# A four-layer block kernel: GpSimd's list in the scan taken in program order, decays moved to the end of a slot, softplus in other buffers, a residual moved; in the latent attention, roots on ScalarE and key masks on GpSimd

## The chip, the cores and the metric

The kernel runs on one core of a Trainium2 chip. A core has TensorE (PE, matrix products and transposes, with separate weight loads PEld), VectorE (DVE), ScalarE (ACT), GpSimd (POOL), SyncE (SP, which here only issues transfers) and 16 DMA engines. Each engine works through its own list of instructions in order and waits at semaphores for the others. The metric is device time in microseconds (us); lower is better.

## The reference, cut to what matters

The input is 32 sequences of 256 tokens with 128 features. Four layers follow each other, each with two halves; every half normalizes, scales and shifts with values drawn from a conditioning vector, does its work, and adds the gated result to `x`. The change touches the first half of layer 0 (a selective scan), the first half of layer 3 (attention whose keys and values come from a narrow latent), and the normalization that opens the second half of layer 3.

```python
h = _layernorm(x, axis=-1) * (1 + ca) + sa
x = x + ga * _L0_attn_ref(h, ...)              # in here:
    xn = (x - mu) * rsqrt(var + EPS) * ln_w + ln_b
    xp = xn @ proj_W.T + proj_b
    def branch(W, b):
        u = softplus(xp @ W.T + b)
        dbc = u @ deltaBC_W.T                  # delta (64), B (16), C (16)
        delta = softplus(delta @ dt_W.T + dt_b)
        h[t] = exp(delta * A) * h[t-1] + (delta * u) * B   # 16 states a feature
        return sum over states of h[t] * C + u * D
    z = xp * sigmoid(xp)
    return branch(fconv) * z + branch(bconv) * z + skip
...
x = x + ga * _L3_attn_ref(h, ...)              # in here:
    q = x @ Wq + bq;  latent = x @ Wl + bl     # latent: 32 features
    k = latent @ Wk + bk;  v = latent @ Wv + bv
    out = softmax(q k^T * SCALE) v;  return out @ Wo + bo
x = x + gb * _L3_ffn_ref(h, ...)               # gated products with blockwise FP4 rounding
```

## The kernel before

The tokens lie in 16 tiles `b` of 512. A stage runs after another; within one, a Python agenda says what is recorded in which slot, and slots are then recorded in order. How that becomes each engine's list differs by engine. Matrix products and transposes (`mm`, `tr`) are kept in program order. In the scan ScalarE's activations are too (`strict_act`); VectorE's and GpSimd's lists there are ordered by a scheduler, by what it takes to be ready first. In the latent attention VectorE is kept in program order (`nc.vector.on`, all shown at line 304), and ScalarE's and GpSimd's lists are the scheduler's.

**The scan** (`scan_layer`). A tile takes 16 slots, and eight groups `p` of two slots: four groups for each of the two branches, four states a group. In slot 2p (`scan_even`) TensorE spreads the inputs into PSUM (`dB`, one buffer of it), and VectorE runs four `tensor_tensor_scan` of 512 (line 875) with the four `decay` tiles. The states then go back through TensorE transposes (`hT`, one PSUM buffer), a ScalarE copy (`hsT`) and products with the spread C (`y<-hsT,Cd`, `scan_weigh`) into one PSUM tile, which ScalarE copies to `yT` after the last group. The decays are exponentials on ScalarE, two a slot (`scan_decay`, ten tiles). A `hT` half of group p is recorded in slot 2p+2 or 2p+3, the decays and the weighing directly behind it, ahead of everything else of the slot.

Everything else prepares later tiles: two normalizations (`norm_rows`, `scan_roots` with the root as Ln and Exp on ScalarE and a Newton step on GpSimd, `norm_scale`), the projections, softplus in two halves (`soft_start` on VectorE, tiles `sp_r` and `sp_m` with one buffer each; `soft_end` on ScalarE and GpSimd), the rows of B and C with a turn through DRAM (`scan_rows`, `far`, `Xc`, and the GpSimd copy `Xr`), their spread forms `Bd` and `Cd` (four GpSimd products each), and after a tile its end: `scan_end` (VectorE `y`, GpSimd `y*z` and `y+h`) and `residual` (VectorE, two instructions into `x`). All side products share one PSUM buffer, `tp`.

**The latent attention** (`latent_attention` in `attention`). A tile takes 16 slots. In each slot TensorE forms one block of scores for the row maximum (`S<-kx,q`, reduced by VectorE into `mt`) and one block for the exponential (`S<-qa,kx`, read by ScalarE into `E`), and the products with the values (`po`). `S` has three PSUM buffers, taken in turn. Ahead of a tile, in slots -14 to -2, come its normalization (`norm_rows`, then `norm_place` with the root by integer start and four Newton steps on VectorE), the latent, the queries, the keys (`keys`: a product of 32 rows with the key weights into a buffer of `S`, then four ScalarE activations that add the bias and mask alternate heads into `kx`) and the values. Behind it come the residual and the same normalization for the next half (`mlp_norm`, tile `fx`) with FP4 rounding on VectorE. The last tile's second normalization is done in the stage after, `fp4_mlp`, where ScalarE is in program order.

Of the kernel before, what the change touches and what calls it, by code (L numbers as in the profile page):

```python
# [30 lines left out]
P = 128  # L31
NSEQ, SEQ = 32, 256
NB = 16
# [107 lines left out]


def rows(v):

    v = np.asarray(v, np.float32).reshape(1, -1)
    return np.broadcast_to(v, (P, v.shape[1]))
# [29 lines left out]
def packs(d):  # L176
# [91 lines left out]
    k.add("Wl", g["Wl"])  # L268
    k.add("Wk", spread(g["Wk"]))
    k.add("Wo", gathered(g["Wo"]))  # L270
    k.add("Wv", np.concatenate([g["Wv"], g["bv"][None]], 0))
    k.add("bq", spread(g["bq"][None])[0].T)
    k.add("kb", key_bias(g["bk"]))
    k.add("bo", col(g["bo"]))
# [32 lines left out]
class Engines:  # L307
    def __init__(self, tc):
        self.nc = tc.nc
        self.vector = InOrder(tc, tc.nc.vector)  # L310

    def __getattr__(self, name):
# [3 lines left out]
class Program:  # L316
# [161 lines left out]

    def norm_newton(self, mv, v, r):


        pool = self.nc.gpsimd
        t = self.wk("ln_t", (P, 4))
        pool.tensor_tensor(t, r, r, ALU.mult)
        pool.tensor_tensor(t, t, v, ALU.mult)
        pool.tensor_scalar(t, t, -0.5, 1.5, ALU.mult, ALU.add)
        pool.tensor_tensor(r, r, t, ALU.mult)
        shift = self.wk("ln_m", (P, 4))
        pool.tensor_tensor(shift, mv[:, :, 0], r, ALU.mult)
        pool.tensor_scalar(shift, shift, -1.0, None, ALU.mult)  # L490
        return r, shift

    def norm_scale(self, xn, r, shift):
# [162 lines left out]
    def scan_layer(self, w):  # L656
# [7 lines left out]
        with ExitStack() as ctx:  # L664
            self.pools(
                ctx, {"dB": 1, "hT": 1, "y": 1, "tp": 1},
                h=4, z=3, dl=3, duT=3, bc=3, xn=1, ln_xn=1, xp=1, y=1, yT=1, rows=1, Xc=1, du=1, sg=1, hsT0=1, hsT1=1, sp_m=1, sp_r=1, Xr=1, mw=1,
            )
            self.strict = self.strict_act = True
            wk = self.wk  # L670
# [16 lines left out]
            def put(t, f, *args):  # L687
                agenda.setdefault(t, []).append((f, args))
# [5 lines left out]
            for n in (1, 2, 3):  # L694
                put(8 * n - 52, lambda n=n: s.update({("mw", n): self.mod_load(n)}))
                put(8 * n - 46, lambda n=n: self.mod_layer(n, s["mw", n], self.ps("y", (P, 6, NSEQ))))
            for p in range(-1, 8 * NB + 3):
                put(2 * p, self.scan_even, s, p)
                put(2 * p + 1, self.scan_odd, s, p)
            for b in range(NB):  # L700
                a = s[b] = {"b": b}
                T = 16 * b
                put(T, self.clear_regions)


                for o, n, src in ((T - 44, 1, lambda a: self.x[a["b"]]), (T - 36, 2, lambda a: a["h"])):
                    put(o, lambda a, n=n, src=src: a.update({("st", n): self.norm_rows(src(a), self.nc.gpsimd)}), a)
                    put(o + 1, lambda a, n=n: self.scan_roots(a, n), a)
                    put(o + 3, lambda a, n=n: self.norm_scale(a["st", n][0], *a["r", n]), a)
                put(T - 40, self.scan_norm_out, a)  # L710
                put(T - 32, self.scan_norm_out2, s, a)
                put(T - 21, self.scan_proj, s, a)
                put(T - 20, self.scan_gate, s, a)
                put(T - 19, self.scan_gate2, s, a)
                for br in (0, 1):
                    o = T + 8 * br
                    put(T - 19 + 6 * br, self.scan_u, s, a, br)
# [12 lines left out]
            self.strict = self.strict_act = False  # L730

# [29 lines left out]

    def soft_start(self, src, bias):

        m, r = self.wk("sp_m"), self.wk("sp_r")
        self.nc.vector.tensor_scalar(r, src, bias, 0.0, ALU.add, ALU.max)
        self.nc.vector.scalar_tensor_tensor(m, r, -2.0, src, ALU.mult, ALU.add)
        return m, r, bias

    def soft_end(self, out, m, r, bias):
        self.act(m, m, AF.Exp, bias=bias)  # L770
        self.act(m, m, AF.Ln, bias=1.0)
        self.nc.gpsimd.tensor_tensor(out, m, r, ALU.add)

    def scan_u(self, s, a, br):
        w = s["w"]
        pu = self.ps("tp")
        self.mm(pu, w.conv[:, br, :], a["xp"])
        a["soft"] = self.soft_start(pu, w.vec[:, 3 + br : 4 + br])

    def scan_u2(self, s, a, br):  # L780
        a["u", br] = self.wk("u")
        self.soft_end(a["u", br], *a["soft"])

    def scan_delta(self, s, a, br):
        pt = self.ps("tp")
        self.mm(pt, s["wd"], a["u", br])
        a["soft"] = self.soft_start(pt, s["w"].vec[:, 5:6])

# [4 lines left out]
    def scan_rows(self, s, a, br):  # L793
# [10 lines left out]
        nc.sync.dma_start(Xc, far.rearrange("n k r -> k n r"))  # L804
        a["Xc"] = self.wk("Xr", (16, 4, 32, 4))
        nc.gpsimd.tensor_copy(a["Xc"].rearrange("k g r n -> k g n r"), Xc.rearrange("k (g n) r -> k g n r", g=4))
        dl = a["dl", br] = self.wk("dl")
        self.soft_end(dl, *a["soft"])
        a["du"] = self.wk("du", (P, 4, 4, 32))
        dq, uq = (t.rearrange("p (q i r) -> p q i r", **cut) for t in (dl, u))  # L810
        nc.gpsimd.tensor_tensor(self.by_chunk(a["du"]), dq, uq, ALU.mult)
        if br:
            a["uu"] = self.wk("uu")
            nc.gpsimd.tensor_tensor(a["uu"], a["u", 0], u, ALU.add)
            nc.gpsimd.tensor_scalar(a["uu"], a["uu"], s["w"].vec[:, 6:7], None, ALU.mult)

# [39 lines left out]
    def scan_even(self, s, p):  # L856
# [48 lines left out]
    def scan_weigh(self, s, p, h):  # L905
# [7 lines left out]
        for i in (0, 1):  # L913
            for q in range(4):
# [5 lines left out]
                    stop=p % 8 == 7 and h == 1 and i == 1,  # L920
                )

    def scan_sum(self, s, a):
# [624 lines left out]
    def keys(self, h, w, bias):  # L1548
# [5 lines left out]
        for x in (0, 1):  # L1554
            for j in (0, 1):
# [5 lines left out]
                    scale=self.c.half[:, j : j + 1],  # L1561
                )
        return k4

# [904 lines left out]
    def latent_attention(self, w):  # L2469
        nc, c = self.nc, self.c  # L2470
        self.mlp_start()
        with ExitStack() as ctx:
# [7 lines left out]
            def before(b, tiles):  # L2480
                t = tiles[b] = {"vz": self.vzs[4 * (b % 2) : 4 * (b % 2) + 4]}

                def head():
                    t["st"] = self.norm_rows(self.x[b])
                    t["norm"] = self.norm_place(*t["st"])

# [16 lines left out]
                def k():  # L2503
                    t["k4"] = self.keys(t["lat"][:32, :], w.Wk, w.kb)

# [316 lines left out]
```

## Time and profile before

| what | us |
|---|---|
| ten runs, median | 6576.51 |
| ten runs, lowest to highest | 6569.2 to 6587.16 |
| the profiled execution, its own time | 6578.39 |
| its span, first to last instruction | 6575.4 |
| first group of scans to the last one of layer 0 | 111.1 to 1079.6 |
| a scan tile in the steady part (scans of group 0 to those of the next tile) | 62.4 |
| the latent attention | about 5488 to 6317 |

A profile row names engine, source line, operation, output and inputs, and a count; in brackets stands how long the engine had been idle before and what ended that. Line 392 is any matrix product, 396 any transpose, 399 any activation through the helper `act`, 304 any VectorE instruction kept in program order; so rows are told apart by the tiles. A wait belongs to the engine that waited. An engine's busy share is a mean over eight stages with different limits, so the two touched stages are read on their own.

### The profile page before, as it was taken

What the parts mean: (1) busy time and instruction counts of PE and PEld (TensorE: products, weight loads), DVE (VectorE), ACT (ScalarE), POOL (GpSimd) and SP (SyncE); (2) the same over time, 40 slices, a digit from 0 to 9 for tenths busy, and PEclk for the clock granted to TensorE, in tenths of its full rate; (3) what the DMA queues carried; (4) which work ended last, traced back from release to release, by engine and by line L of the source; (5) the groups of instructions that cost most, each with busy time, mean ns of one, the idle gap of its engine ahead of it and who ended that gap; (6) DMA issues with size and microseconds to landing.
All of it is one profiled execution on the core that took longest, in us unless ns stands there. A gap on an engine that the chain in (4) does not pass through costs nothing. (4 is left out here: it accounts for less than half of the span.)

```text
span 6575.4 us, 132969 instructions
## 1 busy us (share of the span) xinstructions
PE 5813.9 (88%) x54369; PEld 3298.0 (50%) x54369; DVE 4311.9 (66%) x9937; ACT 3490.6 (53%) x5026; POOL 2660.5 (40%) x2882
## 2 busy tenths in 40 slices
PE   6788886999799999999999777999799998999987
PEld 4555555567465565555655434555322223444444
DVE  4777776621566666665665654888677774777779
ACT  5888884333344444444444432444488885554532
POOL 4555553565444444444543453444245452000000
PEclk7999997899899999999999878999899998998998
DMA  1110110144000000000000101111144441000010
GB/s 63 42 42 29 42 42 33 39 124 130 17 5 6 6 6 5 7 6 5 7 2 2 48 14 28 29 30 27 39 95 91 91 92 36 17 18 17 17 34 30
DMA packets 175877, 232.19 MB, mean 35 GB/s; under 512 B 46567, under 2 KB 95967, under 8 KB 175010
## 3 DMA queue, kind: packets, MB, share of 16 engines
q1 hardware_dynamic: 124880, 126.50, 7.5%
q0 software_dynamic: 26992, 56.62, 3.5%
q10 hardware_dynamic: 23394, 40.58, 1.6%
q8 instruction: 426, 6.98, 0.4%
q14 instruction: 185, 1.52, 0.1%
HBM read 88.22 MB, written 74.97 MB: 25 GB/s over the span
## 5 line engine op out<-in xcount | busy, mean ns | idle before, releaser
L304 DVE TENSOR_REDUCE mt<-S 128x4 f32<-128x1024 f32 (+2 forms) x768 | 756.0, 999 | 508.6 <-PE S L392 505.5
L1438 ACT ACTIVATE E<-S 128x1024 f32<-128x1024 f32 x448 | 458.5, 1024 | 545.9 <-PE S L392 511.1
L875 DVE TENSOR_TENSOR_SCAN hs<-decay,dB 128x512 f32<-128x512 f32 x512 | 582.9, 1203 | 91.7 <-PE dB L392 77.1
L399 ACT ACTIVATE hid<-S,bigw 128x1024 f32<-128x1024 f32 x512 | 537.3, 1111 | 125.5 <-PE S L392 125.3
L1912 POOL TENSOR_SCALAR_AFFINE_SELECT E<-E 128x1024 f32<-128x1024 f32 x320 | 348.7, 1092 | 587.8 <-ACT E L1911 587.3
L304 DVE TENSOR_TENSOR E<-S,cst 128x1024 f32<-128x1024 f32 x320 | 391.2, 1223 | 291.6 <-PE S L392 291.1
L392 PE MATMUL S<-qa,kx 32*128 32x256 f32 x4096 | 538.7, 383 | 34.5 <-DVE mt L304 34.0
L392 PE MATMUL S<-kx,q 32*128 32x512 f32 (+1 forms) x2048 | 528.0, 610 | 17.0 <-ACT kx L1556 16.1
L1911 ACT COPY E<-S 128x1024 f32<-128x1024 f32 x320 | 323.5, 1011 | 327.0 <-PE S L392 315.1
L2459 POOL TENSOR_TENSOR acc<-acc,ye 128x512 f32<-128x512 f32 x256 | 344.5, 1346 | 362.4 <-DVE ye L304 319.6
L392 PEld LDWEIGHTS S<-qa,kx 32*128 32x128 f32 x4096 | 341.5, 190 | 140.2 <-DVE mt L304 104.4
L392 PE MATMUL S<-qG,f 32*128 32x512 f32 x2560 | 368.4, 645 | 47.4 <-DVE E L304 47.4
L392 PE MATMUL S<-hm,bigw 32*128 32x512 f32 x2048 | 340.3, 656 | 25.2 <-ACT hid L399 25.2
L399 ACT ACTIVATE hsT<-hT 128x1024 f32<-128x1024 f32 x256 | 260.8, 1019 | 157.1 <-PE hT L396 156.1
L399 ACT ACTIVATE decay<-dl,A 128x510 f32<-128x510 f32 x512 | 339.1, 715 | 0.0
L396 PE MATMUL hT<-cst,hs 128*128 128x128 f32 x2048 | 295.6, 290 | 22.5 <-ACT hsT L399 21.4
L392 PE MATMUL po<-hid,bigw 128*32 128x512 f32 x2048 | 277.3, 614 | 30.2 <-DVE ye L304 30.2
L1787 ACT ACTIVATE E<-S 128x768 f32<-128x768 f32 (+1 forms) x192 | 169.0, 880 | 237.8 <-PE S L392 237.8
L392 PE MATMUL po<-E,vz 128*32 128x256 f32 x4096 | 294.3, 372 | 0.3 <-ACT oc L1458 0.2
L304 DVE TENSOR_TENSOR ye<-po,gb 128x512 f32<-128x512 f32 x256 | 176.0, 688 | 176.7 <-PE po L392 106.2
L392 PE MATMUL po<-E,vzl 128*32 128x128 f32 x8192 | 276.8, 276 | 0.0
L396 PEld LDWEIGHTS hT<-cst,hs 128*128 128x128 f32 x2048 | 235.0, 147 | 82.4 <-ACT hsT L399 65.1
(530 smaller groups left out, 12930.0 us busy)
## 6 DMA issues: line engine op xcount, KB each, us to landing
gb<-gT SPq DMA_DIRECT2D x256, 256.0 KB
regions<-zeros ACTq DMA_DIRECT2D x16, 2048.0 KB
rx<-far SPq DMA_DIRECT2D x64, 256.0 KB
expert_rows<-eo SPq DMA_DIRECT2D x39, 256.0 KB
xin<-in_x SPq DMA_DIRECT2D x16, 256.0 KB
out<-out SPq DMA_DIRECT2D x16, 256.0 KB
xTd<-xT SPq DMA_DIRECT2D x15, 256.0 KB
xT<-xTd SPq DMA_DIRECT2D x15, 256.0 KB
```

The lines of the kernel that those rows point to most:

```text
L304: return lambda *args, **kw: self.tc.keep_in_program_order(op(*args, **kw))
L392: return self.tc.keep_in_program_order(self.nc.tensor.matmul(out, lhsT, rhs, start=start, stop=stop, **kw))
L396: return self.tc.keep_in_program_order(self.nc.tensor.transpose(out, in_, self.c.ident[:k, :k]))
L399: ins = self.nc.scalar.activation(*args, **kw)
L875: nc.vector.tensor_tensor_scan(hs[:, :, n], decay, dB[:, :, n], 0.0, ALU.mult, ALU.add)
L1438: nc.scalar.activation(e, src, AF.Exp, scale=scale)
L1787: nc.scalar.activation(e, src, AF.Exp, scale=1.0 / math.sqrt(8))
L1911: nc.scalar.copy(e, src)
L1912: nc.gpsimd.affine_select(e, e, [[0, 8], [1, P]], ALU.is_ge, 0.0, base=0, channel_multiplier=-1)
L2459: nc.gpsimd.tensor_tensor(a["acc"], a["acc"], ye, ALU.add)
```

## The change

In the scan, GpSimd's instructions are recorded in program order (`nc.gpsimd.on`). In each slot the two decays and the weighing products are recorded last, behind the side work; the decays are then those of half a group later than before. The copy `yT` is recorded directly behind the last weighing. Softplus writes its first half into the tile that takes the result (`u` or `dl`), so `sp_r` is gone, and `sp_m` has two buffers. The copy `Xr` and the scaling of `uu` are recorded one and two slots after their old place. The residual is recorded in slot T + 25 in place of T + 23.

In the latent attention and `mlp_norm`, the normalization takes its root from Ln and Exp on ScalarE, one Newton step on GpSimd, and four GpSimd instructions to apply it. The key weights carry the bias as a 33rd row; ScalarE copies the product once, and two GpSimd products mask it.

```diff
-    k.add("Wk", spread(g["Wk"]))
+    k.add("Wk", np.concatenate([spread(g["Wk"]), key_row(g["bk"])], 0))
-    k.add("kb", key_bias(g["bk"]))
...
+        self.gpsimd = InOrder(tc, tc.nc.gpsimd)
...
-    def norm_newton(self, mv, v, r):
+    def norm_newton(self, mv, v, r, shifted=True):
...
+        if not shifted:
+            return r, None
...
+    def norm_apart(self, xn, mv, v):
+
+        r = self.norm_roots(v)
+        yield
+        r, _ = self.norm_newton(mv, v, r, False)
+        for n in range(4):
+            self.nc.gpsimd.tensor_scalar(
+                xn[:, n, :], xn[:, n, :], mv[:, n, 0:1], r[:, n : n + 1], ALU.subtract, ALU.mult
+            )
+        yield
...
-                h=4, z=3, dl=3, duT=3, bc=3, xn=1, ln_xn=1, xp=1, y=1, yT=1, rows=1, Xc=1, du=1, sg=1, hsT0=1, hsT1=1, sp_m=1, sp_r=1, Xr=1, mw=1,
+                h=4, z=3, dl=3, duT=3, bc=3, xn=1, ln_xn=1, xp=1, y=1, yT=1, rows=1, Xc=1, du=1, sg=1, hsT0=1, hsT1=1, Xr=1, mw=1,
             )
-            self.strict = self.strict_act = True
+            self.strict = self.strict_act = nc.gpsimd.on = True
...
-            for p in range(-1, 8 * NB + 3):
+            behind = {}
+            for p in range(-2, 8 * NB + 3):
                 put(2 * p, self.scan_even, s, p)
                 put(2 * p + 1, self.scan_odd, s, p)
+                behind[2 * p] = (p + 1, 1), (p - 2, 1)
+                behind[2 * p + 1] = (p + 2, 0), (p - 1, 0)
...
+                    put(o - 13, self.scan_chunks, s, a)
...
-                put(T + 18, self.scan_sum, s, a)
+                put(T - 4, lambda a: nc.gpsimd.tensor_scalar(a["uu"], a["uu"], w.vec[:, 6:7], None, ALU.mult), a)
                 put(T + 21, self.scan_end, s, a)
-                put(T + 23, lambda a: self.residual(0, 0, a["b"], a["y"]), a)
+                put(T + 25, lambda a: self.residual(0, 0, a["b"], a["y"]), a)
             for t in sorted(agenda):
                 for f, args in agenda[t]:
                     f(*args)
+                if t in behind:
+                    decay, sums = behind[t]
+                    self.scan_decay(s, *decay)
+                    self.scan_weigh(s, *sums)
...
-    def soft_start(self, src, bias):
-        m, r = self.wk("sp_m"), self.wk("sp_r")
-        self.nc.vector.tensor_scalar(r, src, bias, 0.0, ALU.add, ALU.max)
-        self.nc.vector.scalar_tensor_tensor(m, r, -2.0, src, ALU.mult, ALU.add)
-        return m, r, bias
+    def soft_start(self, out, src, bias):
+        m = self.wk("sp_m")
+        self.nc.vector.tensor_scalar(out, src, bias, 0.0, ALU.add, ALU.max)
+        self.nc.vector.scalar_tensor_tensor(m, out, -2.0, src, ALU.mult, ALU.add)
+        return out, m, bias
...
-        nc.gpsimd.tensor_copy(a["Xc"].rearrange("k g r n -> k g n r"), Xc.rearrange("k (g n) r -> k g n r", g=4))
...
-            nc.gpsimd.tensor_scalar(a["uu"], a["uu"], s["w"].vec[:, 6:7], None, ALU.mult)
+
+    def scan_chunks(self, s, a):
+        Xc, to = a["rows by chunk"], self.wk("Xr", (16, 4, 32, 4))
+        self.nc.gpsimd.tensor_copy(to.rearrange("k g r n -> k g n r"), Xc.rearrange("k (g n) r -> k g n r", g=4))
+        a["Xc"] = to
...
         self.scan_turned(s, p - 1, 0)
-        self.scan_decay(s, p + 1, 0)
-        self.scan_weigh(s, p - 2, 1)
...
         self.scan_turned(s, p - 1, 1)
-        self.scan_weigh(s, p - 1, 0)
-        self.scan_decay(s, p + 1, 1)
...
+        if p % 8 == 7 and h == 1:
+            self.scan_sum(s, a)
...
+    def masked_keys(self, lat, w):
+
+        pk = self.ps("S", (P, 2, TB))
+        for x in (0, 1):
+            self.mm(pk[:, x, :], w[:, x, :], lat)
+        both = self.wk("kk", (P, 2, TB))
+        self.nc.scalar.copy(both, pk)
+        k4 = self.wk("kx", (P, 2, 2, TB))
+        for x in (0, 1):
+            self.nc.gpsimd.tensor_tensor(
+                k4[:, x],
+                both[:, x, :].unsqueeze(1).to_broadcast([P, 2, TB]),
+                self.c.half.unsqueeze(2).to_broadcast([P, 2, TB]),
+                ALU.mult,
+            )
+        return k4
...
-                    t["st"] = self.norm_rows(self.x[b])
-                    t["norm"] = self.norm_place(*t["st"])
+                    t["st"] = self.norm_rows(self.x[b], nc.gpsimd)
+                    t["norm"] = self.norm_apart(*t["st"])
...
-                    t["k4"] = self.keys(t["lat"][:32, :], w.Wk, w.kb)
+                    t["k4"] = self.masked_keys(t["lat"], w.Wk)
...
-        a["st"] = self.norm_rows(self.x[a["b"]], tag="fx")
-        a["norm"] = self.norm_place(*a["st"])
+        a["st"] = self.norm_rows(self.x[a["b"]], self.nc.gpsimd, "fx")
+        a["norm"] = self.norm_apart(*a["st"])
```

More of the change, by code (lines that the diff above doesn't have):

```diff
@@ L140, in key_bias, with key_row @@
     return out.reshape(4, P).T.reshape(P, 2, 2)
+def key_row(b):
+    full = spread(np.asarray(b)[None]).reshape(1, 2, 8, 16)
+    full[:, :, :, 8] = 1.0
+    return full.reshape(1, 2, P)
 def rows(v):
@@ L729, in scan_layer @@
                     f(*args)
-            self.strict = self.strict_act = False
+                if t in behind:
+                    decay, sums = behind[t]
+                    self.scan_decay(s, *decay)
+                    self.scan_weigh(s, *sums)
+            self.strict = self.strict_act = nc.gpsimd.on = False
     def scan_roots(self, a, n):
@@ L760, in scan_gate2, with soft_end @@
         self.nc.gpsimd.tensor_tensor(a["z"], a["z"], a["xp"], ALU.mult)
-    def soft_start(self, src, bias):
-        m, r = self.wk("sp_m"), self.wk("sp_r")
-        self.nc.vector.tensor_scalar(r, src, bias, 0.0, ALU.add, ALU.max)
-        self.nc.vector.scalar_tensor_tensor(m, r, -2.0, src, ALU.mult, ALU.add)
-        return m, r, bias
-    def soft_end(self, out, m, r, bias):
+    def soft_start(self, out, src, bias):
[3 more added lines that the diff above has]
+        return out, m, bias
+    def soft_end(self, out, m, bias):
         self.act(m, m, AF.Exp, bias=bias)
         self.act(m, m, AF.Ln, bias=1.0)
-        self.nc.gpsimd.tensor_tensor(out, m, r, ALU.add)
+        self.nc.gpsimd.tensor_tensor(out, m, out, ALU.add)
     def scan_u(self, s, a, br):
@@ L777, in scan_u @@
         self.mm(pu, w.conv[:, br, :], a["xp"])
-        a["soft"] = self.soft_start(pu, w.vec[:, 3 + br : 4 + br])
+        a["u", br] = self.wk("u")
+        a["soft"] = self.soft_start(a["u", br], pu, w.vec[:, 3 + br : 4 + br])
     def scan_u2(self, s, a, br):
-        a["u", br] = self.wk("u")
-        self.soft_end(a["u", br], *a["soft"])
+        self.soft_end(*a["soft"])
     def scan_delta(self, s, a, br):
@@ L786, in scan_delta @@
         self.mm(pt, s["wd"], a["u", br])
-        a["soft"] = self.soft_start(pt, s["w"].vec[:, 5:6])
+        a["dl", br] = self.wk("dl")
+        a["soft"] = self.soft_start(a["dl", br], pt, s["w"].vec[:, 5:6])
     def by_chunk(self, t):
@@ L804, in scan_rows @@
         nc.sync.dma_start(Xc, far.rearrange("n k r -> k n r"))
-        a["Xc"] = self.wk("Xr", (16, 4, 32, 4))
-        nc.gpsimd.tensor_copy(a["Xc"].rearrange("k g r n -> k g n r"), Xc.rearrange("k (g n) r -> k g n r", g=4))
-        dl = a["dl", br] = self.wk("dl")
-        self.soft_end(dl, *a["soft"])
+        a["rows by chunk"] = Xc
+        dl = a["dl", br]
+        self.soft_end(*a["soft"])
         a["du"] = self.wk("du", (P, 4, 4, 32))
```

## The prediction

> **What bounds the kernel now.** I read the page for the engines' shares, then the windows view of the two stages that change, then waits, then the timelines of one scan tile (tile 8) and one latent tile.
>
> ```profile
> PE 5813.9 (88%) x54369; PEld 3298.0 (50%) x54369; DVE 4311.9 (66%) x9937; ACT 3490.6 (53%) x5026; POOL 2660.5 (40%) x2882
> ...
> 300.00:600.00 300.00, 243.53 (x3345) 172.52 (x3343) 224.11 (x294) 247.36 (x407) 172.20 (x208) 0.94 0.09 32
> 5490.00:6315.00 825.00, 762.12 (x5943) 382.74 (x5943) 595.68 (x1482) 414.93 (x523) 7.87 (x16) 0.92 0.05 17
> ```
>
> The windows' columns are length, then busy time of PE, PEld, DVE, ACT and POOL. In the scan (first window) no engine is full: PE and ACT stand at 82%, DVE at 75%, so the hand-overs set the time. In the latent attention PE is at 92%: only PE's waits, 63 us in 825, can be won. GpSimd is nearly empty there.
>
> The scan's beat is the distance from one group of four scans to the next. In a steady tile I read, from group 0 to 1 and on to 7 to 0: 8.04, 8.17, 11.25, 6.82, 7.63, 6.00, 8.54, 5.91, sum 62.4. The floor is 5.9: scans 4.55, the spread products `dB` 1.17 into one buffer, hops. What lies above it:
>
> ```profile
> DVE hs L875 <- PE dB L392: 69.0, 41, 2.3
> DVE x L539 <- POOL y L941: 53.9, 14, 3.9
> DVE sp_r L765 <- PE tp L392: 49.0, 27, 2.1
> DVE sp_r L765 <- POOL dl L772: 30.3, 14, 2.2
> ...
> 610.18 0.75 DVE L765 TENSOR_SCALAR sp_r<-tp,w 128x512 f32<-128x512 f32 x1 [2.09 <-PE tp L392]
> 618.28 0.75 DVE L765 TENSOR_SCALAR sp_r<-tp,w 128x512 f32<-128x512 f32 x1 [2.16 <-POOL dl L772]
> 629.75 1.32 DVE L539 SCALAR_TENSOR_TENSOR x<-y,mods,x 128x256 f32<-128x256 f32 x2 [3.84 <-POOL y L941]
> 656.99 0.69 DVE L755 SCALAR_TENSOR_TENSOR sg<-xp,sg 128x512 f32<-128x512 f32 x1 [0.84 <-ACT sg L399]
> ...
> 625.99 1.27 POOL L940 TENSOR_TENSOR y<-y,z 128x512 f32<-128x512 f32 x1 [0.34 <-DVE y L934]
> 627.21 1.27 POOL L814 TENSOR_TENSOR uu<-u 128x512 f32<-128x512 f32 x1
> 628.44 1.27 POOL L941 TENSOR_TENSOR y<-y,h 128x512 f32<-128x512 f32 x1
> ...
> 635.58 2.09 PE L392 MATMUL dB<-Bd,duT 32*128 32x128 f32 x32 [3.96 <-DVE hs L875]
> ```
>
> The first four are waits of 150 to 1000 us: total, times, longest. In front of the scans of group 3 VectorE stands 3.84 us for GpSimd's `y+h`, which has the `uu` add of another tile in front of it; PE is idle meanwhile, and its next `dB` takes 2.09 in place of 1.17. In front of group 2 it stands 2.16 because `sp_r` has one buffer, read by GpSimd.
>
> In the latent attention:
>
> ```profile
> PE S L392 <- DVE mt L304: 33.8, 42, 1.4
> PE S L392 <- ACT kx L1556: 16.1, 16, 1.1
> ...
> 5655.38 1.11 DVE L304 TENSOR_SCALAR ln_xn<-ln_xn,ln_mv,ln_rs 128x128 f32<-128x128 f32 x4
> 5656.41 1.22 DVE L304 TENSOR_REDUCE mt<-S 128x4 f32<-128x1024 f32 x1
> 5657.68 1.13 PE L392 MATMUL S<-qa,kx 32*128 32x256 f32 x8 [1.40 <-DVE mt L304]
> 5679.21 2.78 ACT L1556 ACTIVATE kx<-S,w,cst 128x512 f32<-128x512 f32 x4 [0.91 <-PE S L392]
> 5682.05 0.70 PE L392 MATMUL S<-kx,q 32*128 32x512 f32 x2 [1.07 <-ACT kx L1556]
> ```
>
> The normalization sits in VectorE's list in front of a row maximum, and PE waits 1.40 for the `S` buffer; a second wait, 1.07, is for the four masking activations.
>
> **The scan, edit by edit** (tile gaps). In the changed kernel's lists of instructions the edits do less than the words say. VectorE's list still has `y` and both residual instructions between the scans of groups 2 and 3: its scheduler takes them there whatever slot they are recorded in. PE's order of a period is unchanged in kind. ScalarE now has, in a slot, states, side work, then two decays; `yT` follows the decays.
>
> - 0 to 1: the wait is for `tp` behind ScalarE's `xn`, untouched: 8.05.
> - 1 to 2: the 2.16 wait goes (6.0 would be left), but `yT` is late next. From the scans' start: states' transposes and copy 2.0, softplus half 1.27, decay pair 1.22, `yT` 0.9, hop and weighing products 0.8, `dB` and hop 1.2: 7.4.
> - 2 to 3: GpSimd now does `y+h` directly behind `y*z`: 11.25 − 1.2 = 10.1. PE's idle time falls to about 3.0; I keep `dB` slow.
> - 3 to 4: 6.83. 4 to 5: ScalarE's `h` stands ahead of the decays, 7.3. 5 to 6: PE's own work, 6.2.
> - 6 to 7: `sg` is no longer behind decays (wait 0.84): 7.7.
> - 7 to 0 gets worse. GpSimd's list there is now `dl`, `du`, `Cd` 4.07, `Xr` 1.12, `uu` scaling 1.83, then `ln_v`; before, the scheduler placed `ln_v` when its input came. `dl` starts 3.7 after the scans of group 5, so `ln_v` is done at 3.7 + 1.3 + 1.3 + 1.3 + 4.1 + 1.1 + 1.8 + 0.2 = 14.8 after them, 0.9 after those of group 7 (1.3 ahead of them before). ScalarE's root waits for it, and queued behind the root are decays and the next states copy: root 0.45, decays 1.22, hop and copy 1.05 to 3.6, transposes, rows copy, weighing and `dB` to 7.4, in place of 5.91.
>
> Sum 61.0, so −1.4 in each of 12 steady tiles (−17), and −2 in each of tiles 13 and 14, which have less side work: −21. Bounds: without the late `ln_v` (−1.4 × 12) and with a warm `dB` at 3 to 4 (−0.92 × 13), −21 − 17 − 12 = −50; from the other side +40, in the rivals. `sp_m`'s second buffer and the unneeded `sp_r` cost nothing: no queue gains an instruction. Near the start one weight load moves behind one `Xc` transfer in SP's queue; both land far ahead of use.
>
> The skill's page "TensorE: Matmul & The Clock Gate", Part 1, says that PE falls to half rate after an idle window of about 3.4 us, free-running. By it the 3.0 left would make `dB` 1.17, 12 us less in all; the trace has another `dB`, at 624.35, that took 2.02 after 0.63 of idle, so I keep it slow.
>
> **The latent attention.** VectorE loses two normalizations a tile. Each is 15 small instructions (rows at 162 to 171 ns) and four of 341: 15 × 0.16 + 4 × 0.34 = 3.8 us, 7.6 a tile. VectorE is at 72%, so only what stands in front of a row maximum counts: the 1.40 wait, in 13 tiles (the tiles at the ends differ), −18. The other `mt` waits (0.52 and 0.41) come from FP4 work, which stays. The wait for `kx`: one copy of 1.02 (the row of a 1024-wide activation into `E`) frees `S` 1.76 earlier than 2.78; but the 33-row key product can't lie beside others as the 32-row one did, about +0.5. I take 0.7 of 1.07, ×14 = −10 (0.45 to 1.07: −6 to −15). The first tile's keys come later, +1. Sum −27.
>
> Cover: the roots are two short activations on ScalarE, 50% busy; GpSimd waits for them alone. ScalarE's `E` is put back 1.2 us twice a tile behind the root's wait; the `S` ring hides 1.5. The masks have no row of their own. Nearest: the broadcast product `Cd` 4.07/4 = 1.02 for 512, so 2.1 for each 1024; plain products 1.27, so 2.55. GpSimd has them ready at 5682.5 to 5685.5 of the tile shown, needed at 5686: hidden by 0.5 at worst, PE's wait if it is gone. The four GpSimd applications cost between 1.83/4 = 0.46 and 1.0 each, with 2.8 of slack.
>
> VectorE may be slowed by a busy GpSimd: the residual's row is 698 ns each in the scan and 482 in the latent stage; +0.2 on a few instructions a tile lies in the 0.65 that VectorE has spare in a slot, so I add nothing. The skill's "SBUF — State Buffer", "Who interferes with whom", goes against this change: a VectorE instruction with two SBUF inputs is blocked by a GpSimd one that reads SBUF for its whole length. By that, one block of a mask's length a tile, 16 × 2.3 = +37, would end at 6567.
>
> The tail: the last tile's root in `fp4_mlp` takes 4.1 us from VectorE and adds three table loads to ScalarE (the row there is 1.28): −4.1 + 3.8, 0 within 4.
>
> **Sum.** Against the profiled execution (6578.4; its span 6575.4 and 3.0 around it): 6578.4 − 21 − 27 = 6530. It stands 1.9 above the median of the runs, so 6529 in a run's terms.
>
> **Rivals.**
> - A, the forecast, 6510 to 6552.
> - B, more: `ln_v` is on time (−17), `dB` warm at 3 to 4 (−12), all of the `kx` wait gone (−5): 6529 − 34 = 6495. For it: the root's lateness rests on a chain of eight GpSimd durations with 0.9 at its end. Against: the chain is in list order.
> - C, the scan gains nothing, the latent stage does: 6576.5 − 27 = 6549. For it: VectorE's residual didn't move, and each removed wait has `yT` or `ln_v` close behind.
> - E, the latent stage gains nothing, because masks or port conflicts give back 27, and the scan does: 6576.5 − 21 = 6555.
> - D, slower: the weighing products, now last in a slot, come directly before the next `dB`, which shares PE. Where the states' copy is late (ScalarE has side work ahead of the decays), a pair of weighing products, 0.65, lies on the path that set the beat. In four gaps of a tile and with `yT` 0.5 longer that is +3.1; with the gains of 1 to 2 and 2 to 3 gone behind it, scan +3.1 × 13 = +40; latent −27: 6576.5 + 13 = 6590. It decides once the scan loses more than the latent stage's 27: a tile over 62.4 + 27/13 = 64.5, a mean gap over 8.06. Against: PE is 81% busy, with idle time in most gaps.
>
> **How the numbers follow.** A 0.44, B 0.13, C 0.17, E 0.10, D 0.16. The prediction is A's 6529. The range reaches from B's 6495 to D's 6590, which leaves out half of D and half of B, under 2 in 10: 6494 to 6590. Cases of both signs don't share most of the chance; A alone has 6510 to 6552. A measurement can tell about 0.2%, 13 us: faster is A, B, most of C and E, with a little of each short of it, 0.74; within 0.2% a tenth, from C and E with their losses, 0.09; slower 0.17.
>
> **What would show it.** Right: the wait of VectorE for `dl` gone; residual wait at 2.6 in place of 3.84; `ln_t` on ScalarE waiting for `ln_v` near the scans of group 7; scan tile 61; latent PE waits for `mt` at 1.4 gone, stage 27 shorter. Wrong: a tile over 62.4 with `dB` waiting behind weighing products or `yT` (D); PE waiting for a GpSimd `kx`, or longer VectorE rows beside GpSimd (E); decays named as what the scans wait for, which I price at nothing because ten tiles hold two and a half groups.

## The result, and the profile after

The changed kernel takes 6452.4 us (median of 8 runs, 6448.5 to 6460.4) against 6575.6 for the kernel before (28 runs, 6566.2 to 6587.2). The ratio is 0.9814, 95% interval 0.9806 to 0.9823: 122 us faster, where 48 were forecast and 6494 was the range's lower end. The profiled execution of after took 6450.8 (span 6448.9).

Three landmarks in the two traces say where the time went. The last group of scans starts at 1041.9 in place of 1076.3: −34 (forecast −21). The latent attention, from its first keys to its last exponential, takes 721.7 (5464.3 to 6186.0) in place of 809.4 (5504.6 to 6314.0): −88 (forecast −27). Between the two, the latent stage's first keys are 40 ahead: 34 from the scans and 6 behind them, which I did not trace. The end is +1.5 (forecast 0 within 4). So nearly all that was missed lies in the latent attention.

The page of after, engines' shares:

```profile
PE 5735.3 (89%) x54369; PEld 3278.5 (51%) x54369; DVE 4205.5 (65%) x9329; ACT 3471.7 (54%) x5045; POOL 2861.0 (44%) x3202
```

VectorE loses 106 us of busy time and GpSimd gains 200, as the change says. But PE's busy time also falls, by 79 us, for the same 54369 products. Products cannot become fewer, so they became shorter or overlap more. The granted clock, the share of full speed that PE is given, is the first suspect. The windows view of ten steady latent tiles, before (first fence) and after (second); columns as in the prediction, the third last is the clock:

```profile
5679.20:6188.40 509.20, 471.31 (x3752) 239.61 (x3753) 385.70 (x970) 262.81 (x335) 5.16 (x10) 0.94 0.06 18
```

```profile
5621.70:6071.10 449.40, 438.48 (x3753) 226.68 (x3753) 320.54 (x590) 250.02 (x344) 125.68 (x210) 1.00 0.06 20
```

Sixty microseconds in ten tiles: 33 less PE busy, at a clock of 1.00 in place of 0.94, and 27 less PE idle (38 to 11). PE's waits there, before and then after:

```profile
PE S L392 <- DVE mt L304: 24.4, 29, 1.4
PE S L392 <- ACT kx L1556: 10.7, 10, 1.1
```

```profile
PE S L399 <- DVE mt L310: 7.0, 17, 0.5
```

Both waits of the forecast went, the one for `kx` wholly. In the scan, after's waits of 150 to 1000 us (first fence) and the rows of tile 8 that answer to those of before (second):

```profile
DVE hs L910 <- PE dB L399: 106.3, 77, 4.8
...
DVE x L559 <- POOL y L310: 38.6, 14, 2.8
...
ACT ln_t L406 <- POOL ln_v L310: 20.5, 13, 1.6
PE y L399 <- ACT yT L406: 18.7, 14, 1.3
```

```profile
572.47 4.52 POOL L310 TENSOR_TENSOR Cd<-cst,bc 128x512 f32<-128x512 f32 x4
576.94 1.16 POOL L310 COPY Xr<-Xc 16x512 f32<-16x512 f32 x1
577.99 1.56 POOL L310 TENSOR_SCALAR uu<-uu,w 128x512 f32<-128x512 f32 x1
579.63 0.23 POOL L310 TENSOR_SCALAR ln_v<-ln_mv 128x4 f32<-128x4 f32 x1
579.89 0.20 ACT L406 ACTIVATE ln_t<-ln_v 128x4 f32<-128x4 f32 x1 [1.60 <-POOL ln_v L310]
...
585.49 2.09 PE L399 MATMUL dB<-Bd,duT 32*128 32x128 f32 x32
...
610.97 0.88 DVE L559 SCALAR_TENSOR_TENSOR x<-y,mods,x 128x256 f32<-128x256 f32 x2 [2.75 <-POOL y L310]
...
616.37 2.09 PE L399 MATMUL dB<-Bd,duT 32*128 32x128 f32 x32 [3.49 <-DVE hs L910]
```

The waits for `dl` and for ScalarE's `sg` are gone. The residual wait fell from 3.84 to 2.75 (2.6 forecast), PE behind it is idle for 3.49, and its next `dB` is still slow at 2.09; and the two waits that were named as late next, `yT` and `ln_v`, are there. The distances between scan groups, read from VectorE's timeline as in the prediction, means of tiles 1 to 12:

| from, to | 0,1 | 1,2 | 2,3 | 3,4 | 4,5 | 5,6 | 6,7 | 7,0 | tile |
|---|---|---|---|---|---|---|---|---|---|
| before | 8.04 | 8.18 | 11.25 | 6.82 | 7.66 | 6.00 | 8.53 | 5.91 | 62.4 |
| forecast | 8.05 | 7.4 | 10.1 | 6.83 | 7.3 | 6.2 | 7.7 | 7.4 | 61.0 |
| after | 7.20 | 7.40 | 9.72 | 6.65 | 7.06 | 6.00 | 7.77 | 8.31 | 60.1 |

### The profile page after: what moved, and what is told of

It is laid out like the page before. It is cut to its first block, busy times and chain, and to the rows that moved or that the text cites. A ratio compares the mean times of both kernels' runs of the same rounds, so it can differ in the third digit from the quotient of the medians.

```text
span 6448.9 us, 132602 instructions
## 1 busy us (share of the span) xinstructions
PE 5735.3 (89%) x54369; PEld 3278.5 (51%) x54369; DVE 4205.5 (65%) x9329; ACT 3471.7 (54%) x5045; POOL 2861.0 (44%) x3202
## 5 line engine op out<-in xcount | busy, mean ns | idle before, releaser
L399 PE MATMUL S<-qa,kx 32*128 32x256 f32 x4096 | 510.1, 371 | 12.1 <-DVE mt L310 11.5
L399 PE MATMUL S<-kx,q 32*128 32x512 f32 (+1 forms) x2048 | 509.2, 590 | 3.0 <-POOL kx L1607 2.7
L399 PEld LDWEIGHTS S<-qa,kx 32*128 32x128 f32 x4096 | 326.0, 185 | 94.9 <-DVE mt L310 62.6
```

The lines of the kernel that those rows point to most:

```text
L399: return self.tc.keep_in_program_order(self.nc.tensor.matmul(out, lhsT, rhs, start=start, stop=stop, **kw))
```

## The experiments

Each time was taken against runs of the kernel before on the same chip, so ratios are compared. Chips differ: one gave before 6647, the others 6573 to 6577. "Against after" means the difference of the ratios (after is 0.9814); a hundredth is 66 us. Every experiment is a single profile and a few runs, so differences under some 10 us are not told apart.

### Each half alone

`scan_only` is before with the scan's edits; `latent_only` is before with the latent stage's.

> The scan's edits alone, with the latent attention of before. In the changed kernel the last scan group of layer 0 comes 34 us earlier and the stage after it some 5 us more. If the two parts are independent: 6575 - 39 = 6536, 34 of it inside the scan stage, a steady tile of 60.2 as in the changed kernel. If something of the latent stage's gain came from the scan's edits (another DMA or POOL order further on), the time is below 6525.

> The latent attention's edits alone, with the scan of before. If the parts are independent: 6575 - 87 = 6488, and PE's granted clock 1.00 in the steady tiles of the latent stage, where before had 0.94. If the gain there needs the scan's edits, it falls short of -87.

Measured: 0.9952 (0.9939 to 0.9965), −32 us; and 0.9883 (0.9865 to 0.9900), −77 us. The sum, −109, is near after's −122 within both intervals; the traces agree better: in `scan_only` the first latent keys are 40 us earlier, and in `latent_only` the ten tiles are as after has them:

```profile
5666.20:6115.60 449.40, 438.50 (x3753) 226.40 (x3757) 320.40 (x590) 250.04 (x345) 125.65 (x210) 1.00 0.06 20
```

The halves are independent, and the clock of 1.00 needs nothing of the scan.

### The latent stage's two parts alone

```diff
# keys_only: before, and
-                    t["k4"] = self.keys(t["lat"][:32, :], w.Wk, w.kb)
+                    t["k4"] = self.masked_keys(t["lat"], w.Wk)
# norms_only: before, and (also in mlp_norm, with tag "fx")
-                    t["st"] = self.norm_rows(self.x[b])
-                    t["norm"] = self.norm_place(*t["st"])
+                    t["st"] = self.norm_rows(self.x[b], nc.gpsimd)
+                    t["norm"] = self.norm_apart(*t["st"])
```

> Only the masked keys (one ScalarE copy, two GpSimd products); scan and normalization as before. In ten steady latent tiles the changed kernel is 60 us shorter: 27 less PE idle, 33 less PE busy at a clock of 1.00 in place of 0.94. Clock theory (a PE wait of 1.07 to 1.40 also sets off some us at half clock): the kx wait's 1.07 x 15 = -16 and a part of the clock's loss with it, -30 to -55, clock between 0.94 and 1.00. Rival, waits alone (the clock goes its own way): -16, clock still 0.94. My prediction's term was -10.

> Only the roots on ScalarE and the normalization on GpSimd in the latent stage; scan and keys as before. Clock theory: the mt wait's 1.40 x 15 = -21 and a part of the clock's loss with it, -35 to -65, clock between 0.94 and 1.00. Rival, waits alone: -21, clock 0.94. My prediction's term was -18. If the two parts alone sum to much less than the 87 of both, each wait is by itself enough to lose the clock.

Measured: keys 0.9986 (0.9976 to 0.9996), −9 us; normalization 0.9890 (0.9873 to 0.9906), −72 us. Ten steady tiles of `keys_only` (first fence) and `norms_only` (second):

```profile
5671.90:6174.80 502.90, 474.46 (x3753) 236.84 (x3757) 384.52 (x970) 246.18 (x304) 42.61 (x30) 0.95 0.06 18
```

```profile
5654.98:6113.00 458.02, 436.88 (x3751) 229.33 (x3750) 321.29 (x590) 266.86 (x374) 88.55 (x190) 0.99 0.06 20
```

Neither theory got both right. The keys come near the wait alone, as the rival said and as the prediction had it (−10). That does not show that the `kx` wait costs no clock: it was followed by half clock in four of 14 tiles of before, in `norms_only` in one. Single executions spread by as much as this term: in the two profiles the stage is 17 us shorter with the keys alone, and the ten tiles only 6. The normalization is worth more than the clock theory's upper end: with the `kx` wait still there (1.07 in each of these tiles) the clock is 0.99. So the 1.40 wait for `mt` is the one that PE pays for, several times over. Two adjacent tiles of before show one part of how:

```profile
5727.35:5775.49 48.14, 44.65 (x376) 22.77 (x375) 37.41 (x94) 26.14 (x33) 0.52 (x1) 1.00 0.06 19
5775.49:5828.41 52.92, 49.98 (x376) 25.74 (x375) 37.50 (x94) 26.14 (x33) 0.52 (x1) 0.87 0.05 17
```

The same 376 products, 4.8 us apart, and the only difference is a clock of 0.87. In some tiles a wait is followed by several microseconds at half clock, in others not; the next section shows which. The price without that is read from tiles at clock 1.00: 48.1 before, 47.6 with the keys alone, 45.2 with the normalization alone, 44.7 with both. So the normalization gives 2.95 a tile at full clock, though PE's wait was 1.40. PE's timeline of before around that wait, and two pairs of products a little later:

```profile
5752.97 1.13 PE L392 MATMUL S<-kx,q 32*128 32x512 f32 x4
5755.49 1.13 PE L392 MATMUL S<-qa,kx 32*128 32x256 f32 x8 [1.40 <-DVE mt L304]
...
5757.71 0.70 PE L392 MATMUL S<-kx,q 32*128 32x512 f32 x2
5757.72 0.70 PE L392 MATMUL S<-qa,kx 32*128 32x256 f32 x4
```

The products for the maximum and for the exponential have 32 rows each; where both buffers are free they run side by side (0.01 apart). Where the second waits, the first runs alone, and the period loses the overlap too: from one product of values (`po<-E,vz`) to the next this period takes 4.52 in before and 2.44 in `norms_only`, 2.08 for a wait of 1.40. The other 0.87 lies in four periods in which PE never stood idle, but the second product again started late beside the first. That is in the waits of the weight loads, ten tiles of before and of `norms_only`:

```profile
PEld S L392 <- DVE mt L304: 63.8, 61, 2.2
```

```profile
PEld S L392 <- DVE mt L304: 24.7, 30, 1.3
```

They fall by 39 us and by 31 waits, where PE's own row fell by 18 (24.4 to 6.5).

### The same wait put back without the normalization

A tax of eight VectorE instructions whose result nothing reads is added to after, once at the place of the old normalization and once in an idle stretch:

```diff
+                def tax():
+                    pad = wk("pad", (P, P))
+                    for n in range(8):
+                        nc.vector.tensor_scalar(pad, c.ident, 1.0, 0.0, ALU.subtract, ALU.mult)
...
-                return [(-13, part, "last"), (-12, part, "last")] + [(*work, "late") for work in works]
+                return [(-13, part, "last"), (-12, part, "last"), (-12, tax, "last")] + [(*work, "late") for work in works]
# tax_in_gap: slot -4 in place of -12
```

> The changed kernel with eight idle-run VectorE instructions of 128x128 (2.2 us together, into a scratch tile that nothing reads) once a latent tile, at the place where before did the end of the normalization, ahead of a row maximum; nothing left out. Rival, the wait as PE's row shows it: PE waits about 1.4 again, 16 x 1.4 = +22 against the changed kernel. Clock and overlap theory: the wait costs 2.1 in the period itself (the two products of a period no longer overlap) and in most tiles sets off a stretch at half clock that costs 2 to 5: +45 to +75, granted clock back at about 0.95.

> The same eight instructions eight slots later, where VectorE of the changed kernel is idle 2.5 ahead of a row maximum; nothing left out. All theories in which VectorE's work costs only through a row maximum that comes late: 0 within 5 against the changed kernel, clock 1.00. If VectorE's work as such slows the stage (ports, power and so the clock), it costs like the other place.

Measured: 0.9889 (0.9873 to 0.9906), +49 us against after; and 0.9844 (0.9827 to 0.9860), +20. Two tiles of `tax_at_wait`, one behind the other (44.7 each in after):

```profile
5694.40:5740.93 46.53, 44.38 (x378) 22.52 (x379) 32.49 (x64) 24.88 (x35) 12.60 (x21) 1.00 0.06 20
5740.93:5790.33 49.40, 47.29 (x378) 23.75 (x378) 32.56 (x64) 24.91 (x34) 12.61 (x21) 0.93 0.06 18
```

PE's wait is 1.16 in both. In the first it costs 1.84 at full clock, in the second 4.7. Together they bear out the theory of clock and overlap; the rival's +22 is short of the interval, +39 to +60.

Why the same wait costs clock in one tile and not in the other can be read from the same trace. The clock changes only at borders that lie 3.41 us apart. The stretches between such borders around the two waits (5720.52 to 5721.68, and 5767.04 to 5768.20), with PE's busy time, clock, DMA share and GB/s:

```profile
5717.32:5720.73 3.41, 3.20 (x30) 1.00 0.06 12
5720.73:5724.15 3.42, 2.47 (x24) 1.00 0.00 0
...
5765.11:5768.52 3.41, 2.25 (x16) 1.00 0.03 5
5768.52:5771.93 3.41, 3.41 (x20) 0.50 0.03 5
5771.93:5775.34 3.41, 3.41 (x21) 0.50 0.22 77
5775.34:5778.76 3.42, 3.42 (x37) 1.00 0.00 0
```

A border cuts the first wait into 0.21 and 0.95, and the clock stays at 1.00. The second wait lies whole between two borders, and from the next border on the clock is at half. The latent stages of before, `keys_only` and `tax_at_wait`, from the third tile on, have 45 waits for `mt` of 1.15 to 1.40. All 29 that lie whole between two borders were followed by half clock. Of the 16 that are cut, none of the 12 whose longer part is under 1.1 was, and three of the four with 1.19 to 1.26.

The tax in the gap was expected to cost nothing, and in twelve of the fifteen distances from one tile's keys to the next's it does cost nothing (44.68 in the steady ones, as in after). The three others take 53.1, 53.1 and 52.2 in place of 45.6, 45.5 and 44.9, which is the whole +20. They are neighbours, at the tiles in which VectorE also quantizes the next stage's weights (rows of `qw_xn` or `qd_xn` stand directly ahead of the tax); there the tax fell beside GpSimd's masks. VectorE, GpSimd and PE of `tax_in_gap`, one of the three tiles:

```profile
5803.99 5.35 DVE L310 TENSOR_SCALAR pad<-cst 128x128 f32<-128x128 f32 x8
```

```profile
5804.99 3.74 POOL L1607 TENSOR_TENSOR kx<-kk,cst 128x1024 f32<-128x1024 f32 x2 [9.69 <-ACT kk L1604]
```

```profile
5810.53 2.08 PE L399 MATMUL S<-qa,kx 32*128 32x256 f32 x8 [3.60 <-DVE mt L310]
```

Elsewhere the eight take 2.04 together. Here they take 5.35: two of them take 1.942 and 1.814, each about as long as one mask (1.89). The row maximum came 3.3 us late, PE waited 3.60, and the tile's clock was 0.90. So in these tiles VectorE's work by itself cost nothing; it cost where it makes a row maximum late, and two masks of GpSimd lengthened it by some three microseconds.

### The scan: the late root and the residual

```diff
# scale_late: after, and
-                put(T - 4, lambda a: nc.gpsimd.tensor_scalar(a["uu"], a["uu"], w.vec[:, 6:7], None, ALU.mult), a)
+                put(T + 1, lambda a: nc.gpsimd.tensor_scalar(a["uu"], a["uu"], w.vec[:, 6:7], None, ALU.mult), a)
# residual_late: after, and
-                nc.vector.tensor_tensor_scan(hs[:, :, n], decay, dB[:, :, n], 0.0, ALU.mult, ALU.add)
+                with nc.vector.kept():
+                    nc.vector.tensor_tensor_scan(hs[:, :, n], decay, dB[:, :, n], 0.0, ALU.mult, ALU.add)
-                put(T + 25, lambda a: self.residual(0, 0, a["b"], a["y"]), a)
+                put(T + 27, self.scan_residual, a)      # the residual, kept in order as well
# both_late: both
```

> The changed kernel with GpSimd's scaling of uu recorded five slots later, in an idle stretch of GpSimd; nothing left out. The changed kernel's scan tile has 7.4 to 9.4 from group 7 to 0 (mean 8.4, before 5.91), which I put down to ln_v standing behind that scaling (1.6 to 1.8) in GpSimd's list, ScalarE's root waiting 1.60 for it and PE falling to half clock. If so: 7 to 0 at 5.9 to 6.3, 0 to 1 back at 8.0 in every tile, net -1.5 a tile, -15 to -25 in all against the changed kernel (6452): about 6432. Rival: yT, decays or PE's own list set that gap: 7 to 0 stays above 7.4 and the time within 6 of 6452.

> The changed kernel with VectorE's scans and residual kept in program order and the residual recorded in slot T + 27, so that VectorE does it between the scans of groups 5 and 6; nothing left out. In the changed kernel VectorE still does it ahead of the scans of group 3 and waits 2.75 for GpSimd. If that wait is on the path: 2 to 3 falls from 9.72 to about 6.3 and 3 to 4 from 6.6 to about 6.1 (dB at full clock): -3.5 to -4.0 in 14 tiles, -45 to -55 against 6452. Rival: ScalarE, busy 51.5 of 60 a tile, takes over as the limit: -15 to -25.

> Both of the last two edits. If they are independent the sum, -60 to -75 against the changed kernel, about 6385; a scan tile near 55. If ScalarE becomes the limit at some 54 to 56 a tile, -45 to -60.

Measured: 0.9780 (0.9760 to 0.9800), −22 us against after; 0.9737 (0.9715 to 0.9759), −51; 0.9693 (0.9671 to 0.9715), −80 (interval −94 to −65), where −60 to −75 was expected if the two are independent. In the traces the last group of scans starts 29, 62 and 83 us earlier than in after. The distances of a typical tile, with two more experiments that come below:

| from, to | 0,1 | 1,2 | 2,3 | 3,4 | 4,5 | 5,6 | 6,7 | 7,0 | tile |
|---|---|---|---|---|---|---|---|---|---|
| after (mean) | 7.20 | 7.40 | 9.72 | 6.65 | 7.06 | 6.00 | 7.77 | 8.31 | 60.1 |
| scale_late | 7.98 | 7.40 | 9.71 | 6.04 | 7.03 | 6.00 | 7.77 | 6.00 | 57.9 |
| residual_late (mean tile) | 6.1 to 8.0 | 7.40 | 6.17 | 5.95 | 6.76 | 6.74 | 8.13 | 6.6 to 9.2 | 55.7 |
| both_late | 7.27 | 7.40 | 6.16 | 5.95 | 6.76 | 6.75 | 8.13 | 5.91 | 54.3 |
| decays_early | 8.70 | 6.77 | 11.17 | 6.83 | 7.64 | 6.00 | 8.64 | 6.37 | 62.1 |
| gpsimd_free | 7.81 | 7.41 | 11.27 | 6.82 | 6.45 to 7.56 | 6.00 | 7.77 | 5.92 | 59.9 |

With the scaling elsewhere, 7 to 0 falls from 8.31 to 6.00 and `dB` there to 1.17. ScalarE of `scale_late` at the same place shows the root without a wait, which is why no bracket stands behind it:

```profile
561.29 0.62 ACT L406 ACTIVATE z<-sg 128x512 f32<-128x512 f32 x1
562.06 0.21 ACT L406 ACTIVATE ln_t<-ln_v 128x4 f32<-128x4 f32 x1
```

With VectorE kept in order, the residual leaves the place ahead of group 3, and 2 to 3 falls from 9.72 to 6.17. VectorE of `residual_late`, where it went:

```profile
578.04 0.66 DVE L972 TENSOR_TENSOR y<-uu,tp 128x512 f32<-128x512 f32 x1
578.69 4.59 DVE L310 TENSOR_TENSOR_SCAN hs<-decay,dB 128x512 f32<-128x512 f32 x4
...
595.87 2.35 DVE L310 SCALAR_TENSOR_TENSOR x<-y,mods,x 128x256 f32<-128x256 f32 x2
```

This is the largest gain of the scan, and it was in reach of the change's own words: the agenda's slot for the residual moved, but not VectorE's list. (The experiment also records it two slots later still; the slot alone was not tried.) Together the two edits give a version that beats both kernels, 0.9693 of before.

### Decays early, and GpSimd free

`decays_early` is after with the two decays and the weighing recorded directly behind the scans and transposes again; `gpsimd_free` is after without `nc.gpsimd.on = True` in the scan.

```diff
# decays_early
                 for f, args in agenda[t]:
                     f(*args)
-                if t in behind:
-                    decay, sums = behind[t]
-                    self.scan_decay(s, *decay)
-                    self.scan_weigh(s, *sums)
+                    if f in (self.scan_even, self.scan_odd):
+                        decay, sums = behind[t]
+                        self.scan_decay(s, *decay)
+                        self.scan_weigh(s, *sums)
```

> The changed kernel with decays and weighing products recorded where before had them, directly behind the scans and transposes, ahead of the slot's side work (the group that each decay serves stays as changed); nothing left out. My step: the move to the slot's end frees sg (0.8 from 6 to 7) and h (0.3 from 4 to 5) and puts yT behind decays (+1.4 from 1 to 2). Undone: 6 to 7 at 8.5, 4 to 5 at 7.4, 7 to 0 the same 8.4 as GpSimd's list is the same: a tile +1 to +2, +10 to +25 against the changed kernel. Rival: decays early also keep the scans and PE fed, so that 7 to 0 falls with them: 0 to -15.

> The changed kernel with GpSimd's list in the scan ordered by the scheduler again; nothing left out. My steps: program order took the uu add from between y*z and y+h (1.2 to 1.5 from 2 to 3) and put ln_v late (+2.5 from 7 to 0, with PE cold). Undone: 2 to 3 at 10.9, 7 to 0 at 6, 0 to 1 at 8: net within 12 of the changed kernel, -10 to +5. Rival, program order carries most of the scan's gain: +20 to +35.

Measured: 0.9853 (0.9836 to 0.9869), +26 us against after; 0.9824 (0.9808 to 0.9840), +7 with an interval that holds 0. The order of a slot carries the scan's gain: without it a tile takes 62.1, nearly before's 62.4. One distance went against the expectation: 7 to 0 fell to 6.37, though GpSimd's list was the same. ScalarE still waits 1.57 there for `ln_v`, but with the decays ahead of it the late root held up less; so that loss needed two edits, the late `ln_v` and the decays last. GpSimd's program order gives 1.6 from 2 to 3, as the `uu` add no longer stands between `y*z` and `y+h`, and takes 2.4 from 7 to 0: even, as its expectation said.

### yT ahead of the decays

`yt_first` is `both_late` with the last weighing of a tile and `yT` recorded directly behind that slot's scans:

```diff
+                first = t in behind and t % 16 == 2
                 for f, args in agenda[t]:
                     f(*args)
+                    if first and f == self.scan_even:
+                        self.scan_weigh(s, *behind[t][1])
```

> The kernel with both late edits, and in the one slot of a tile where the last weighing of the tile before stands, that weighing and yT recorded directly behind the scans, ahead of the softplus half and the decays; nothing left out. My step from 1 to 2 (7.4: copy, softplus half, two decays, then yT, then weighing and dB) says: 1 to 2 falls from 7.40 to 6.0 to 6.3, a tile from 54.3 to about 53.1, -12 to -18 against both late edits. Rival: another of ScalarE's instructions is late at that place in yT's stead: 0 to -4.

Measured: 0.9699 (0.9683 to 0.9715), no better than `both_late`. From 1 to 2 it does fall, 7.40 to 6.00, which shows the step; but 2 to 3 rises from 6.16 to 6.78 and 3 to 4 from 5.95 to 6.89, a tile 54.5. The time is given back at the next root: ScalarE waits 1.1 for `ln_v`, which GpSimd does only behind `Cd`, `Xr` and `u`, whose start did not move. From the waits of `yt_first` between 610 and 630 us:

```profile
ACT ln_t L406 <- POOL ln_v L310: 1.1, 1, 1.1
```

## Why the prediction was wrong

The direction and both places were right; the size was not, and one term carries the error.

**The latent stage's normalization, −18 forecast, −72 measured: the step that failed.** "The 1.40 wait, in 13 tiles" took PE's idle time as the price of a late row maximum, and counted one such wait a tile. Four things were left out. The wait also ends the overlap of two 32-row products: 2.1 for 1.40 in its own period. Late row maxima that leave PE busy with one product alone do not show in PE's row at all, but in that of the weight loads: 0.9 a tile. Then PE's clock: a wait that lay whole in one stretch of 3.41 us was followed by one to three such stretches at half speed. And three tiles, those in which VectorE quantizes the next stage's weights, had a second wait for `mt` of 1.21 to 1.28, which went with the normalization as well. With the last two a tile of before took 51 on average where one at full clock takes 48.1; with the normalization gone it is 45.8 against 45.2. In sum (2.95 + 2.8 − 0.6) = 5.2 a tile, or some 70 in 13 to 14 tiles. The clock gate was weighed in the prediction, but for the scan's `dB` alone; the row that would have told it stood in the first windows view, a clock of 0.92 in a stage with PE at 92%.

**The keys, −10 forecast, −9 measured (−3 to −16).** 1.07 less some 0.5 for the 33-row product that lies alone; a tile at full clock gives 0.5. The masks take 1.89 each (2.1 to 2.55 estimated), the applications on GpSimd 0.79 (0.46 to 1.0), and neither is waited for, but in the first tile, where PE waits 2.69 for a mask. In the tiles of the normalization alone the wait of 1.07 was still there, at a clock of 0.99. The term left the clock out here too; that the total still fits is in part luck, as the four times that before lost clock behind this wait show.

**The scan, −21 forecast, −34 measured.** That VectorE's list keeps the residual ahead of group 3, that `yT` is late next (7.4 against 7.40), that the `uu` add goes from 2 to 3, that `sg` is freed (7.7 against 7.77), and that `ln_v` comes late, were right, and the experiments on the scan show them. Mis-sized were 7 to 0 (7.4, measured 7.4 to 9.4: PE went idle for 1.97 at the worse ones and did the next products at half clock, which I had not priced), and 0 to 1 (8.05, measured 6.6 to 8.0: after a long 7 to 0 the next distance is short; I take it that the side work is done by then). 2 to 3 and 4 to 5 gave 0.4 and 0.2 more than forecast, and tiles 13 and 14 gave 3.8 and 2.7 where 2 each was forecast.

**The Trainium skill's "SBUF — State Buffer", "Who interferes with whom"**, was weighed at +37 for masks that block VectorE. Nothing of the sort is in after: what stands in VectorE's list beside the masks are above all row maxima that read PSUM, and they take 1.23 beside a mask as elsewhere. So my placing of the cost was wrong. Where an experiment put VectorE instructions that read and write SBUF there, two were held for 1.94 and 1.81, about a mask's length each. They have one SBUF input, so they do not test the rule on two inputs that was weighed. That section also says that a `tensor_scalar`, which they are, can contend in a mode that uses both ports; in which mode these ran, no row here shows. The residual does have two inputs: its two instructions took 2.35 beside GpSimd products in `residual_late` and 0.88 in after, which agrees with the rule.

**The rivals.** B named more gain, but from other sources (`ln_v` on time, `dB` warm, the rest of `kx`), and ended 40 us above the result. D's mechanism did not decide: weighing last stood in front of `dB` in each period, but the distances fell.

The profiled execution against the runs, 1.9 above the median then, 1.6 below it for after, mattered for nothing here.

## What to carry to other kernels

Where PE is over 90% busy in a stage, price a wait not by PE's idle row alone: read the waits of the weight loads, look whether the products on either side of the wait otherwise run side by side, and compare the same tile's length at full and at reduced clock; here a wait of 1.4 us was worth 3 a tile at full clock and some 5 with the clock that it cost. Ask also how long a wait is: here those of 1.15 us or more took the clock down unless a border cut them, and most shorter ones did not. A new slot in an agenda moves an instruction only on engines that keep the recorded order, so look in each engine's list whether it moved; here the one that did not was worth 51 us. And after each wait taken away, look in the list of every other engine for what stands in front of the next one: of the changes tried in the scan, one gave back at the following root all it had won.

## What the runs showed of the hardware

- In the latent stage PE's granted clock changed only at borders 3.41 us apart. Waits of 1.15 to 1.40 us whole between two borders were followed by half clock in 29 of 29 cases, for one to three stretches; waits cut by a border into parts under 1.1 in none of 12. In `tax_at_wait` a stretch that was busy for 2.25 of its 3.41 was enough for half clock behind it, one that was busy for 2.47 was not.
- A wait of 1.07 for `kx` lies close to that limit. Whole between two borders, it was followed by half clock in four of 12 cases in before and in one of eight in `norms_only`. What decides those isn't settled by these runs.
- The Trainium skill's "TensorE: Matmul & The Clock Gate", Part 1, has a free-running window of about 3.4 us, with which the 3.41 here agree. It puts half rate behind an idle window; here a window with about a third of idle time was enough.
- VectorE instructions from SBUF to SBUF that met a GpSimd product took about as long as the product: 1.942 and 1.814 in place of 0.227, beside masks of 1.89. Two residual instructions of 0.88 together took 2.35 beside two GpSimd products of 1.28 and 1.34 in `residual_late`.
